# In-degrees from a stationary tile of ones, and keys of a fourth weight tile between the last transposes

## The chip, the cores and the metric

The kernel runs on one core of a Trainium2 chip. The metric is the device time of one execution in microseconds; the time before is the median of three runs. A separate execution was profiled, and every row quoted below is from it. Engines are called as the profile calls them: PE is TensorE's matmul, PEld its weight load, DVE is VectorE, ACT is ScalarE, POOL is GpSimd, SP is SyncE, whose queue issues most transfers.

## The reference

One layer of a graph network: 625 nodes of 1024 features in float32, and 20000 edges sorted by their destination. The layer's input is normalised, then two branches are added to it (a two-layer GraphSAGE and a linear attention), then a mixture of experts. What the change touches is the normalisation, the keys of the attention and the in-degrees:

```python
xn = _layernorm(x, axis=-1)
# graph branch
deg = segment_sum(ones, edge_dst, N)
deg_inv = 1.0 / maximum(deg, 1.0)
h = relu(sage(xn, src, dst, deg_inv, W_self0, W_neigh0, b0))
out = sage(h, src, dst, deg_inv, W_self1, W_neigh1, b1)
# sage: h @ W_self + (segment_sum(h[src], dst) * deg_inv[:, None]) @ W_neigh + b
# attention branch, 16 heads of 64
k = softmax(xn @ Wk over the nodes); q = softmax(xn @ Wq over a head) / 8
context = k^T v per head; attn = q context; attn @ Wo + bo
```

## The kernel before

**Numbers.** TensorE works in a float32 form of reduced precision, so each operand is split into a high and a low part (`split`: ScalarE casts the high part, VectorE subtracts it to get the low one), and each product is three products: high by high, high by low, low by high. Weights stream in tiles of 128x1024 (`Stream.next`, three raw and three split buffers); a load is issued as soon as a raw buffer has been split.

**Start.** The 625 nodes are five token tiles, four of 128 and one of 113 rows. For each, `first_stats` (VectorE) takes mean and variance, `first_scale` (VectorE, with a square root on ScalarE) turns them into scale and bias, `first_norm` normalises on VectorE or ScalarE, and `first_turn` transposes the tile on TensorE in two groups of four blocks (into `pst`) and splits it into `xnh` and `xnl`, with the features on partitions. The order of all these is written out by hand and kept on each engine (`keep`). While the last three token tiles are being prepared, TensorE multiplies the first three weight tiles of the keys with the first two token tiles: `keys_steps`, a step being half of a weight tile's features over some columns, 12 products. Here these are 256 columns (two token tiles); the remaining 370 columns of these three weight tiles follow behind the transposes.

**Keys and counting.** The steps go on through the eight tiles of Wk and the eight of W_self0 (columns 384 and 242 from the fourth tile on), each key tile being exponentiated (`keys_exp`) and transposed back (`keys_back`). `kbuf` is a ring of three key tiles. Between the steps VectorE builds one-hot rows of the edges (`one_hots`), of which TensorE makes the matrix of edge counts between source and destination (`count_group`, `pa`), with five source tiles packed into one number. `unpack` takes it apart into `ath`: source nodes on partitions, destinations along the row.

**In-degrees.** After the first half of the queries, `queries_step` runs between the quarters of the second half: it transposes the finished `q` of the first half, then in the first quarter calls `degrees` and in the second `look`. `degrees` multiplies each block of `ath` (as the stationary operand) with two columns of ones (`two`), so that the degrees of a destination tile stand on partitions; 25 products. `inverse_degrees` takes the reciprocal of the 128x5 result with one correction step (`recip`). `look` sums the degrees over everything and takes a maximum, and leaves in `rare` whether the packed counting may have overflowed; if so a slow path recounts, and all engines read `rare` before the attention's output. During the second half of the values, `inverse` spreads the inverse degrees over a row on all partitions (`dinv`) with five transposes and two copies on ScalarE. `dinv` scales the first layer's sums, `degs[:, 2]` the second layer's.

**Order.** PSUM has eight banks, handed out in turn under one tag; the queries' and the values' halves each hold five of them (`accs`). The scheduler orders each engine's instructions by priority except where they are kept; each engine runs its own in order.

Of the kernel before, what the change touches and what calls it, by code (L numbers as in the profile page):

```python
# [73 lines left out]
def gps_layer(ctx: ExitStack, tc: tile.TileContext, x, src, dst,  # L74
# [20 lines left out]
    def bank(name="ps"):  # L95
        return psum.tile([128, 512], F32, name=name, tag="ps")
# [5 lines left out]
    class Stream:  # L102
# [24 lines left out]
                self.raw[self.loaded] = r  # L127
                self.loaded += 1

        def next(self, eng=None, **order):  # L130
            if self.ready:
                return self.ready.pop(0)
            i = self.used
            self.used += 1
            self.load(max(i + self.ahead, i + 1))
            ap = self.todo[i]
            r = self.raw.pop(i)
            if self.pair is not None:
# [186 lines left out]
    def first_scale(a, b):  # L325
        inv_std(lnv[:T, a:b, 1], *(lnt[:T, i, a:b] for i in range(3)), order=keep)
        keep(nc.vector.scalar_tensor_tensor(lnt[:T, 1, a:b], lnv[:T, a:b, 0], -1.0, lnt[:T, 0, a:b],
                                            op0=ALU.mult, op1=ALU.mult))
# [26 lines left out]
        nc.tensor.transpose(psf[:, :EP], edges[:, 1, 0:1].to_broadcast([EP, 128]), ident[:EP, :EP])  # L355
        keep(nc.scalar.copy(first_dst, psf[:, :EP].rearrange("p (g j) -> p g j", g=NG)[:, :, 0]))

    shared = big.tile([128, 8 * NP], F32, name="shared", tag="big")
    kbuf = shared[:, 5 * NP:].rearrange("p (i s) -> p i s", s=NP)


    ksum = const.tile([128, KT], F32, name="ksum")
# [1 line left out]
    kscr = const.tile([128, KT], F32, name="kscr")  # L364

    def keys_back(o):
        ke = kbuf[:, o % 3, :N]
        for t0, n in ((0, NT - 1), (NT - 1, 1)):
            ps = bank("pskt").rearrange("p (a b) -> p a b", b=128)
            p = rows(t0)  # L370
            for t in range(n):
                nc.tensor.transpose(ps[p, t, :], ke[:, cols(t0 + t)], ident)
            nc.scalar.copy(knat[p, t0:t0 + n, o * 128:(o + 1) * 128], ps[p, :n, :])

    def keys_exp(o):
        ke = kbuf[:, o % 3, :N]
# [6 lines left out]

    def keys_step(s):
        o, i, h = s // 4, s // 2 % 2, s % 2
        if s < 12:
            o, i = s // 2 % 3, s // 6
        if (o, i, h) == (1, 1, 0):
            wks[3] = st.next()
        if i == 0 and h == 0 and 2 < o < 2 * KT - 1:  # L390
            wks[o + 1] = st.next()
        if h == 0:
            kps[0] = bank("psk")
        wh, wl = wks[o]
        c0, n = ((0, 2 * T), (2 * T, NP - 2 * T))[i] if o < 3 else SPARTS[i]
        c, ps = slice(c0, c0 + n), kps[0]
        for kt in range(4 * h, 4 * h + 4):
            nc.tensor.matmul(ps[:, :n], wh[:, kt, :], xnh[:, kt, c], start=kt == 0, stop=False)  # L398
            nc.tensor.matmul(ps[:, :n], wh[:, kt, :], xnl[:, kt, c], start=False, stop=False)  # L399
            nc.tensor.matmul(ps[:, :n], wl[:, kt, :], xnh[:, kt, c], start=False, stop=kt == KT - 1)  # L400
        if h == 1:
            n = min(n, N - c0)
            if o < KT:
                nc.scalar.copy(kbuf[:, o % 3, c0:c0 + n], ps[:, :n])
# [6 lines left out]
    def keys_steps(n):  # L411
        for _ in range(n):
            k = ks[0]
            ks[0] += 1
            if 8 <= k < 4 * KT + 8 and k % 4 == 0:
                keys_exp((k - 8) // 4)
            if 12 <= k < 4 * KT + 12 and k % 4 == 0:
                keys_back((k - 12) // 4)
            if k < 8 * KT:
                keys_step(k)  # L420

    def keys_weights(o):
        wks[o] = st.next(order=keep)


    with tc.high_priority():
        first_stats(0)
        first_stats(1)
        first_scale(0, 2)
        first_norm(0, nc.vector)  # L430
        keys_weights(0)
        first_norm(1, nc.scalar)
        first_turn(0)
        first_turn(1)
        first_stats(2)
        keys_weights(1)
        keep(nc.scalar.copy(edges, ei))
        keys_weights(2)
        keys_steps(2)
        turn_edges()  # L440
        keys_steps(2)
        first_stats(3)
        first_scale(2, 4)
        first_norm(2, nc.scalar)
        first_norm(3, nc.vector)
        keys_steps(2)
        first_stats(4)
        first_scale(4, 5)
        first_turn(2)
        first_norm(4, nc.scalar)  # L450
        first_turn(3)
        last = first_turn(4)


# [60 lines left out]
    knat = slot_n("knat")  # L515
    hself = slot_t("hself", F32)

    placed = 0
# [30 lines left out]
    def inverse_degrees():  # L549
        nc.vector.tensor_scalar(degs[:T, 1, :], degs[:T, 0, :], 1.0, None, op0=ALU.max)  # L550
        recip(degs[:T, 2, :], degs[:T, 1, :], degs[:T, 3, :])

    def degrees():
        ps = bank("psdg")
        for t in range(NT):
            for s in range(NT):
                nc.tensor.matmul(ps[rows(t), 2 * t:2 * t + 2], ath[rows(s), s, cols(t)], two[rows(s)],
                                 start=s == 0, stop=s == NT - 1)
        for a, b in ((0, NT - 1), (NT - 1, NT)):
            nc.vector.tensor_copy(degs[rows(a), 0, a:b],  # L560
                                  ps[rows(a), 2 * a:2 * b].rearrange("p (t k) -> p t k", k=2)[:, :, 0])
        inverse_degrees()

    rare = const.tile([1, 1], I32, name="rare")

    def look():


        nc.vector.reduce_sum(degs[:T, 4, 0:1], degs[:T, 0, :], axis=AX.X)
        ps = bank("psdm").rearrange("p (a b) -> p a b", b=128)  # L570
        for k in range(2):
            nc.tensor.transpose(ps[:1, k, :T], degs[:T, 4, k:k + 1], ident[:T, :T])
        few = const.tile([1, 2], F32, name="few")
        nc.vector.reduce_sum(few[:, 0:1], ps[:1, 0, :T], axis=AX.X)
        nc.vector.reduce_max(few[:, 1:2], ps[:1, 1, :T], axis=AX.X)
        nc.vector.tensor_scalar(few[:, 0:1], few[:, 0:1], float(E), None, op0=ALU.is_lt)
        nc.vector.scalar_tensor_tensor(rare, few[:, 1:2], 16.0, few[:, 0:1], op0=ALU.is_ge, op1=ALU.add)

    ard = dram.tile([NT * WIN, NP], F32, name="ard")
    atd = dram.tile([N, NP], F32R, name="atd")  # L580
# [1 line left out]
    def recount():  # L582
# [34 lines left out]
        for t in range(NT):  # L617
            pt = bank("psdt")
            for s in range(NT):
                al = tmp.tile([128, T], F32R, name="al", tag="tmp")  # L620
                nc.gpsimd.dma_start(al[rows(s), rows(t)], atd[cols(s), cols(t)])
                nc.tensor.matmul(pt[rows(t), :2], ath[rows(s), s, cols(t)], two[rows(s)], start=s == 0, stop=False)
                nc.tensor.matmul(pt[rows(t), :2], al[rows(s), rows(t)], two[rows(s)], start=False, stop=s == NT - 1)
            nc.vector.tensor_copy(degs[rows(t), 0, t:t + 1], pt[rows(t), 0:1])
        inverse_degrees()

# [76 lines left out]
    mid_ctx = ExitStack()  # L703
    midp = mid_ctx.enter_context(tc.tile_pool(name="midp", bufs=1))
    dinv = midp.tile([128, NP], F32, name="dinv")
# [618 lines left out]
```

## Time and profile before

| | |
|---|---|
| median of 3 runs | 1019.87 us (1019.27 to 1020.14) |
| profiled execution, whole | 1021.48 us |
| profiled execution, span from the first to the last instruction | 1019.5 us |
| mean granted TensorE clock | 0.998 |
| `degrees` on TensorE | 179.89 to 182.62 us |
| `look` on TensorE (two transposes) | 192.04 to 192.18 us |
| `inverse` on TensorE | 256.17 and 263.43 us |

A row of the timeline gives start and duration in us, engine, line, operation, the names written and read, the shapes, and in brackets the idle time before it and what ended that. Durations of a product include its tail, which lies beside the next one; the pace of products is read from the distance of their starts.

### The profile page before, as it was taken

The numbers are of one execution on the slowest core, as the hardware profiler recorded it, in microseconds if no ns is written. First come the engines' busy times: TensorE is split into PE (matmuls) and PEld (weight loads), VectorE is DVE, ScalarE is ACT, GpSimd is POOL, SyncE is SP. The second block draws the span as 40 slices with busy tenths as digits, with TensorE's granted clock in tenths as the row PEclk, the third lists the DMA queues.
The fourth block names the chain that finished last, engine by engine and source line by source line (L and its number), as shares of the span: only waits on it lengthen the run. The fifth ranks groups of instructions, "written<-read, shape, count | busy, mean of one in ns | idle before, by whom it ended". The sixth has DMA issues, their size and how long they took to land. (4 is left out here: it accounts for less than half of the span.)

```text
span 1019.5 us, 14780 instructions
## 1 busy us (share of the span) xinstructions
PE 999.7 (98%) x5557; PEld 862.4 (85%) x5557; DVE 595.5 (58%) x1207; ACT 394.7 (39%) x579; POOL 150.5 (15%) x206
## 2 busy tenths in 40 slices
PE   9999999999999999999999999999999989999998
PEld 6899998888888888888878999997978777887786
DVE  7999735462532335432337364458676788887681
ACT  4443232232311123122116242345646576766610
POOL 1000011110145100200001004103030043210130
PEclk9999999999999999999999999999999999999999
DMA  7122227574225421322220128476877798887961
GB/s 231 42 84 63 84 83 247 189 254 140 95 83 183 133 78 48 122 83 82 79 68 2 55 72 285 123 202 201 271 241 224 262 311 276 293 286 257 332 247 51
DMA packets 111464, 164.68 MB, mean 162 GB/s; under 512 B 5931, under 2 KB 63443, under 8 KB 111382
## 3 DMA queue, kind: packets, MB, share of 16 engines
q1 hardware_dynamic: 97734, 118.38, 36.9%
q0 software_dynamic: 13456, 45.08, 13.4%
q8 instruction: 47, 0.77, 0.3%
q14 instruction: 35, 0.29, 0.1%
q10 hardware_dynamic: 192, 0.16, 0.0%
HBM read 133.19 MB, written 30.42 MB: 160 GB/s over the span
## 5 line engine op out<-in xcount | busy, mean ns | idle before, releaser
L99 DVE TENSOR_TENSOR wlo<-wraw,whi 128x1024 fp32r<-128x1024 f32 x149 | 187.8, 1261 | 265.4 <-ACT whi L99 261.2
L99 ACT CAST whi<-wraw 128x1024 fp32r<-128x1024 f32 x149 | 156.6, 1051 | 286.1 <-PE psg L210 66.2
L1162 PE MATMUL pse<-xs,whi 128*128 128x448 f32 (+1 forms) x384 | 108.9, 357 | 0.0
L99 DVE TENSOR_TENSOR wlo<-wmore,whi 128x1024 fp32r<-128x1024 f32 x67 | 86.9, 1296 | 28.6 <-ACT whi L99 27.3
L1158 PE MATMUL pse<-xs,wlo 128*128 128x224 f32 (+1 forms) x384 | 89.6, 254 | 0.0
L99 ACT CAST whi<-wmore 128x1024 fp32r<-128x1024 f32 x67 | 70.4, 1051 | 48.4 <-PE psz L210 18.5
L398 PE MATMUL psk<-xnh,whi 128*128 128x384 f32 (+3 forms) x256 | 79.1, 313 | 0.4 <-ACT xnh L99 0.3
L399 PE MATMUL psk<-xnl,whi 128*128 128x384 f32 (+3 forms) x256 | 77.8, 307 | 0.8 <-DVE xnl L99 0.8
L400 PE MATMUL psk<-xnh,wlo 128*128 128x384 f32 (+3 forms) x256 | 77.7, 306 | 0.0
L1214 PE MATMUL psy<-wlo,he 128*128 128x512 f32 (+1 forms) x176 | 70.0, 398 | 3.3 <-DVE wlo L99 2.9
L1158 PEld LDWEIGHTS pse<-xs,wlo 128*128 128x128 f32 x384 | 72.0, 190 | 1.0
L1162 PEld LDWEIGHTS pse<-xs,whi 128*128 128x128 f32 x384 | 69.0, 189 | 2.4
L1213 PE MATMUL psy<-whi,he 128*128 128x512 f32 (+1 forms) x176 | 69.5, 395 | 0.0
L1215 PE MATMUL psy<-whi,he 128*128 128x512 f32 (+1 forms) x176 | 69.1, 392 | 0.0
L99 POOL TENSOR_TENSOR xs<-raw,xs 128x512 fp32r<-128x512 f32 (+2 forms) x24 | 35.5, 1501 | 118.9 <-ACT xs L99 98.6
L399 PEld LDWEIGHTS psk<-xnl,whi 128*128 128x128 f32 x256 | 48.5, 190 | 1.3 <-DVE xnl L99 1.3
L478 DVE TENSOR_SCALAR hot<-iota,srow,unit 125x128 f16<-125x128 f16 x160 | 49.4, 311 | 0.0
L398 PEld LDWEIGHTS psk<-xnh,whi 128*128 128x128 f32 x256 | 48.4, 190 | 0.9 <-ACT xnh L99 0.9
L400 PEld LDWEIGHTS psk<-xnh,wlo 128*128 128x128 f32 x256 | 48.4, 189 | 0.0
L1214 PEld LDWEIGHTS psy<-wlo,he 128*128 128x128 f32 (+1 forms) x176 | 31.8, 180 | 14.8 <-DVE wlo L99 6.6
L477 DVE TENSOR_SCALAR hot<-iota,edt 125x128 f16<-125x128 f16 x160 | 39.6, 251 | 4.1 <-PE pa L495 3.8
L1213 PEld LDWEIGHTS psy<-whi,he 128*128 128x128 f32 (+1 forms) x176 | 31.9, 181 | 10.1
(347 smaller groups left out, 2328.3 us busy)
## 6 DMA issues: line engine op xcount, KB each, us to landing
wraw<-in_L_ffn_w_dram SPq DMA_DIRECT2D x65, 512.0 KB, 5.0
wmore<-in_L_ffn_w_dram SPq DMA_DIRECT2D x63, 512.0 KB, 5.3
xsd<-zt POOLq DMA_DIRECT2D x9, 1024.0 KB
wraw<-in_L_gnn_W_self_dram SPq DMA_DIRECT2D x16, 512.0 KB, 3.8
wraw<-in_L_gnn_W_neigh_dram SPq DMA_DIRECT2D x16, 512.0 KB, 3.7
wraw<-_ffn_shared_gate_up_dram SPq DMA_DIRECT2D x16, 512.0 KB, 3.8
wraw<-in_L_mix_Wk_dram SPq DMA_DIRECT2D x8, 512.0 KB, 7.0
wraw<-in_L_mix_Wq_dram SPq DMA_DIRECT2D x8, 512.0 KB, 3.6
```

The source lines that it names most:

```text
L99: return (order(nc.scalar.copy(hi, srcap)), order((eng or nc.vector).tensor_sub(lo, srcap, hi.bitcast(F32))))
L398: nc.tensor.matmul(ps[:, :n], wh[:, kt, :], xnh[:, kt, c], start=kt == 0, stop=False)
L399: nc.tensor.matmul(ps[:, :n], wh[:, kt, :], xnl[:, kt, c], start=False, stop=False)
L400: nc.tensor.matmul(ps[:, :n], wl[:, kt, :], xnh[:, kt, c], start=False, stop=kt == KT - 1)
L477: nc.vector.tensor_scalar(h[:ET, :WIN], iota[:ET, :WIN], edst[e], None, op0=ALU.is_equal)
L478: return nc.vector.tensor_scalar(h[:ET, WIN:], iota[:ET, :WIN], srow[e], unit[e].bitcast(F32), op0=ALU.is_equal, op1=ALU.mult)
L1158: nc.tensor.matmul(ps[a][:, :n], wl[:, k, c], xs[:, kt, 0, :], start=False, stop=False)
L1162: nc.tensor.matmul(ps[a][:, :2 * n], wh[:, k, c], xs[:, kt], start=kt == 0, stop=kt == KT - 1)
L1213: nc.tensor.matmul(acc, h(kt, 0), wh[:, k, :], start=kt == 0, stop=False)
L1214: nc.tensor.matmul(acc, h(kt, 0), wl[:, k, :], start=False, stop=False)
L1215: nc.tensor.matmul(acc, h(kt, 1), wh[:, k, :], start=False, stop=kt == KT - 1)
```

## The change

Two things are changed. The in-degrees are made with a stationary tile of ones and `ath` as the moving operand, so that each sum comes out on all 128 partitions at once, along the row; the reciprocal is taken there, 128x314 and 128x312, and is `dinv` directly. `degrees` moves from the first to the third quarter of the queries' second half; `look` moves to the end of the values' first half, and now also turns `dinv` back into a column for `degs[:, 2]`. `inverse` is left for the slow path only.

At the start, a fourth weight tile of the keys is split early, into a buffer of its own (`fourth`), and its 256 early columns are multiplied in two steps between the transposes of the last three token tiles. `kbuf` becomes a ring of four in a buffer of its own, `keys_exp` and `keys_back` come two steps later, and the normalisation of the fifth token tile is placed ahead of the third one's transposes. The slot `knat` is taken earlier, and the one-hot rows begin with eight groups of four and not six.

```diff
-        def next(self, eng=None, **order):
+        def next(self, eng=None, into=None, **order):
...
-            if self.pair is not None:
+            if into is not None:
+                hi, lo = into
+            elif self.pair is not None:
...
-    shared = big.tile([128, 8 * NP], F32, name="shared", tag="big")
-    kbuf = shared[:, 5 * NP:].rearrange("p (i s) -> p i s", s=NP)
+    kbuf = big.tile([128, 4, NP], F32, name="kbuf", tag="big")
+
+    fourth = big.tile([128, 2, D], F32R, name="fourth", tag="big")
...
     def keys_step(s):
         o, i, h = s // 4, s // 2 % 2, s % 2
-        if s < 12:
-            o, i = s // 2 % 3, s // 6
+        if s < 16:
+            o, i = s // 2 % 4, s // 8
         if (o, i, h) == (1, 1, 0):
-            wks[3] = st.next()
-        if i == 0 and h == 0 and 2 < o < 2 * KT - 1:
+            wks[4] = st.next()
+        if i == 0 and h == 0 and 3 < o < 2 * KT - 1:
             wks[o + 1] = st.next()
...
-        c0, n = ((0, 2 * T), (2 * T, NP - 2 * T))[i] if o < 3 else SPARTS[i]
+        c0, n = ((0, 2 * T), (2 * T, NP - 2 * T))[i] if o < 4 else SPARTS[i]
...
-            if 8 <= k < 4 * KT + 8 and k % 4 == 0:
-                keys_exp((k - 8) // 4)
-            if 12 <= k < 4 * KT + 12 and k % 4 == 0:
-                keys_back((k - 12) // 4)
+            if 10 <= k < 4 * KT + 10 and k % 4 == 2:
+                keys_exp((k - 10) // 4)
+            if 14 <= k < 4 * KT + 14 and k % 4 == 2:
+                keys_back((k - 14) // 4)
...
     def keys_weights(o):
-        wks[o] = st.next(order=keep)
+        wks[o] = st.next(into=(fourth[:, 0, :], fourth[:, 1, :]) if o == 3 else None, order=keep)
...
         keys_steps(2)
         turn_edges()
-        keys_steps(2)
         first_stats(3)
         first_scale(2, 4)
         first_norm(2, nc.scalar)
         first_norm(3, nc.vector)
-        keys_steps(2)
+        keys_weights(3)
+        keys_steps(4)
         first_stats(4)
         first_scale(4, 5)
+        first_norm(4, nc.scalar)
         first_turn(2)
-        first_norm(4, nc.scalar)
+        keys_steps(1)
         first_turn(3)
+        keys_steps(1)
         last = first_turn(4)
...
+    knat = slot_n("knat")
     with tc.high_priority():
-        for _ in range(6):
+        for _ in range(8):
             keys_steps(1)
...
-    two = const.tile([128, 2], F32R, name="two")
-    nc.vector.memset(two.bitcast(F32), 1.0)
+    ones = const.tile([128, 128], F32R, name="ones")
+    nc.vector.memset(ones.bitcast(F32), 1.0)
+    dinv = const.tile([128, NP], F32, name="dinv")
...
     def degrees():
-        ps = bank("psdg")
-        for t in range(NT):
-            for s in range(NT):
-                nc.tensor.matmul(ps[rows(t), 2 * t:2 * t + 2], ath[rows(s), s, cols(t)], two[rows(s)],
-                                 start=s == 0, stop=s == NT - 1)
-        for a, b in ((0, NT - 1), (NT - 1, NT)):
-            nc.vector.tensor_copy(degs[rows(a), 0, a:b],
-                                  ps[rows(a), 2 * a:2 * b].rearrange("p (t k) -> p t k", k=2)[:, :, 0])
-        inverse_degrees()
+        for i, (c0, n) in enumerate(PARTS):
+            ps = bank("psdg")
+            for s in range(NT):
+                nc.tensor.matmul(ps[:, :n], ones[rows(s), :], ath[rows(s), s, c0:c0 + n], start=s == 0, stop=s == NT - 1)
+            nc.vector.reduce_sum(few[:, i:i + 1], ps[:1, :n], axis=AX.X)
+            deg = tmp.tile([128, 2, PARTS[0][1]], F32, name="deg", tag="tmp")
+            nc.vector.tensor_scalar(deg[:, 0, :n], ps[:, :n], 1.0, None, op0=ALU.max)
+            recip(dinv[:, c0:c0 + n], deg[:, 0, :n], deg[:, 1, :n])
...
     def look():
-        nc.vector.reduce_sum(degs[:T, 4, 0:1], degs[:T, 0, :], axis=AX.X)
-        ps = bank("psdm").rearrange("p (a b) -> p a b", b=128)
-        for k in range(2):
-            nc.tensor.transpose(ps[:1, k, :T], degs[:T, 4, k:k + 1], ident[:T, :T])
...
+        ps = bank("psdm")
+        for t in range(NT):
+            nc.tensor.transpose(ps[rows(t), t:t + 1], dinv[:1, cols(t)], ident[:1, :1])
+        for a, b in ((0, NT - 1), (NT - 1, NT)):
+            nc.vector.tensor_copy(degs[rows(a), 2, a:b], ps[rows(a), a:b])
+        nc.tensor.transpose(ps[:1, 128:128 + T], degs[:T, 4, 1:2], ident[:T, :T])
+        nc.vector.reduce_max(few[:, 2:3], ps[:1, 128:128 + T], axis=AX.X)
+        nc.vector.tensor_add(few[:, 0:1], few[:, 0:1], few[:, 1:2])
...
     def queries_step(u):
...
-        if u == 0:
+        if u == 2:
             degrees()
-        elif u == 1:
-            look()
...
     def values_step(half, u):
         if half == 0:
...
-        elif u > 1:
-            inverse(*((0, NT - 1), (NT - 1, 1))[u - 2])
+            if u == 3:
+                look()
```

More of the change, by code (lines that the diff above doesn't have):

```diff
@@ L366, in keys_back @@
     def keys_back(o):
-        ke = kbuf[:, o % 3, :N]
+        ke = kbuf[:, o % 4, :N]
         for t0, n in ((0, NT - 1), (NT - 1, 1)):
@@ L375, in keys_exp @@
     def keys_exp(o):
-        ke = kbuf[:, o % 3, :N]
+        ke = kbuf[:, o % 4, :N]
         mx = small.tile([128, 2], F32, name="mx")
@@ L403, in keys_step @@
             if o < KT:
-                nc.scalar.copy(kbuf[:, o % 3, c0:c0 + n], ps[:, :n])
+                nc.scalar.copy(kbuf[:, o % 4, c0:c0 + n], ps[:, :n])
             else:
@@ L514, in gps_layer @@
                 one_hots(4)
-    knat = slot_n("knat")
     hself = slot_t("hself", F32)
@@ L551, in inverse_degrees @@
         recip(degs[:T, 2, :], degs[:T, 1, :], degs[:T, 3, :])
+    few = const.tile([1, 4], F32, name="few")
     def degrees():
-        ps = bank("psdg")
-        for t in range(NT):
+        for i, (c0, n) in enumerate(PARTS):
+            ps = bank("psdg")
             for s in range(NT):
-                nc.tensor.matmul(ps[rows(t), 2 * t:2 * t + 2], ath[rows(s), s, cols(t)], two[rows(s)],
-                                 start=s == 0, stop=s == NT - 1)
-        for a, b in ((0, NT - 1), (NT - 1, NT)):
-            nc.vector.tensor_copy(degs[rows(a), 0, a:b],
-                                  ps[rows(a), 2 * a:2 * b].rearrange("p (t k) -> p t k", k=2)[:, :, 0])
@@ L566, in look @@
     def look():
-        nc.vector.reduce_sum(degs[:T, 4, 0:1], degs[:T, 0, :], axis=AX.X)
-        ps = bank("psdm").rearrange("p (a b) -> p a b", b=128)
-        for k in range(2):
-            nc.tensor.transpose(ps[:1, k, :T], degs[:T, 4, k:k + 1], ident[:T, :T])
-        few = const.tile([1, 2], F32, name="few")
-        nc.vector.reduce_sum(few[:, 0:1], ps[:1, 0, :T], axis=AX.X)
-        nc.vector.reduce_max(few[:, 1:2], ps[:1, 1, :T], axis=AX.X)
+        ps = bank("psdm")
+        for t in range(NT):
+            nc.tensor.transpose(ps[rows(t), t:t + 1], dinv[:1, cols(t)], ident[:1, :1])
@@ L576, in look @@
+        for a, b in ((0, NT - 1), (NT - 1, NT)):
[3 more added lines that the diff above has]
+        nc.vector.tensor_add(few[:, 0:1], few[:, 0:1], few[:, 1:2])
         nc.vector.tensor_scalar(few[:, 0:1], few[:, 0:1], float(E), None, op0=ALU.is_lt)
-        nc.vector.scalar_tensor_tensor(rare, few[:, 1:2], 16.0, few[:, 0:1], op0=ALU.is_ge, op1=ALU.add)
+        nc.vector.scalar_tensor_tensor(rare, few[:, 2:3], 16.0, few[:, 0:1], op0=ALU.is_ge, op1=ALU.add)
@@ L621, in recount @@
                 nc.gpsimd.dma_start(al[rows(s), rows(t)], atd[cols(s), cols(t)])
-                nc.tensor.matmul(pt[rows(t), :2], ath[rows(s), s, cols(t)], two[rows(s)], start=s == 0, stop=False)
-                nc.tensor.matmul(pt[rows(t), :2], al[rows(s), rows(t)], two[rows(s)], start=False, stop=s == NT - 1)
+                nc.tensor.matmul(pt[rows(t), :2], ath[rows(s), s, cols(t)], ones[rows(s), :2], start=s == 0, stop=False)
+                nc.tensor.matmul(pt[rows(t), :2], al[rows(s), rows(t)], ones[rows(s), :2], start=False, stop=s == NT - 1)
             nc.vector.tensor_copy(degs[rows(t), 0, t:t + 1], pt[rows(t), 0:1])
@@ L704, in gps_layer @@
     midp = mid_ctx.enter_context(tc.tile_pool(name="midp", bufs=1))
-    dinv = midp.tile([128, NP], F32, name="dinv")
     def values_step(half, u):
```

## The prediction

> **What bounds the kernel now.** I read the page's busy shares first: TensorE is busy for nearly the whole span, so only what shortens TensorE's own queue, or fills a hole in it, moves the end.
>
> ```profile
> span 1019.5 us, 14780 instructions
> PE 999.7 (98%) x5557; PEld 862.4 (85%) x5557; DVE 595.5 (58%) x1207; ACT 394.7 (39%) x579; POOL 150.5 (15%) x206
> ```
>
> So I went to the two places that the change touches. The first is the start, in TensorE's timeline (start, duration, line, idle time before it) and then ScalarE's:
>
> ```profile
> 23.21 0.28 PE L400 MATMUL psk<-xnh,wlo 128*128 128x256 f32 x1
> 23.54 1.97 PE L282 MATMUL pst<-ident,xts 128*128 128x128 f32 x16
> 27.12 0.70 PE L282 MATMUL pst<-ident,xts 113*128 113x113 f32 x5 [1.62 <-ACT xts L336]
> ...
> 27.91 0.51 PE L282 MATMUL pst<-ident,xts 113*128 113x113 f32 x3
> 28.52 0.77 PE L398 MATMUL psk<-xnh,whi 128*128 128x370 f32 x3
> 29.53 0.44 PE L399 MATMUL psk<-xnl,whi 128*128 128x370 f32 x1 [0.23 <-DVE xnl L99]
> ```
>
> ```profile
> 25.83 1.24 ACT L336 ACTIVATE xts<-xts,lnt 113x1024 f32<-113x1024 f32 x1
> 26.98 2.02 ACT L99 CAST xnh<-pst 128x512 fp32r<-128x512 f32 x4
> ```
>
> The early keys run out at 23.33. Until the keys of the other columns run steadily, about 29.0 (29.53 less three products of 0.17 started early), only 24 transposes of 0.11 and a small one run: 2.75 of 5.7 us. Some 2.9 us are lost, mostly to the fifth tile's normalisation on ScalarE.
>
> The second place is the in-degrees: TensorE's timeline, then the same stretch by windows (per window: busy time of PE, PEld, DVE, ACT, POOL, then the granted clock and DMA).
>
> ```profile
> 179.10 1.03 PE L669 MATMUL psqt<-ident,q 128*128 128x128 f32 x8
> 179.89 2.87 PE L557 MATMUL psdg<-two,ath 128*128 128x2 f32 x25
> 182.62 0.47 PE L208 MATMUL psq<-whi,xnh 128*128 128x512 f32 x1
> ...
> 185.90 0.63 PE L208 MATMUL psq<-whi,xnh 128*128 128x512 f32 x1
> ```
>
> ```profile
> 180.00:182.00 2.00, 2.00 (x21) 2.00 (x20) 1.62 (x4) 1.88 (x4) 0.30 (x1) 1.00 0.56 197
> 182.00:184.00 2.00, 2.00 (x13) 1.78 (x13) 1.20 (x5) 0.00 (x0) 0.00 (x0) 0.86 1.03 276
> 184.00:186.00 2.00, 2.00 (x6) 1.52 (x6) 2.00 (x10) 0.00 (x0) 0.00 (x0) 0.50 0.93 301
> 186.00:188.00 2.00, 2.00 (x9) 1.59 (x8) 0.29 (x3) 0.00 (x0) 0.47 (x2) 0.78 0.78 256
> ```
>
> 25 products with two moving columns hold TensorE from 179.89 to 182.62, 2.73 us or 0.109 each. Right behind them the granted clock is halved. From 183.40 to 187.04 nine products of 512 columns take 3.64 us, where 0.227 each (187.04 to 187.27, and so on) would make 2.04: 1.60 us lost. It is the one clear dip of the clock in the trace.
>
> **The change, part by part.**
>
> *In-degrees.* Removed from TensorE: the 25 narrow products, 2.73; the two transposes of `look`, 0.14; and in `inverse` four transposes that push the next product from 256.17 to 256.52, 0.35, and one of 0.10. Added: ten products with 314 or 312 moving columns. The products of 256 columns start 0.120 apart (14.80 to 14.92), those of 370 0.170 apart (29.97 to 30.14); a line between gives 0.145, so 1.45 us. `look` now has six tiny transposes: by the narrow products 0.109 each, by the old ones 0.07; I take 0.65 us. Together -3.42 + 2.10 = -1.32 us. The dense products also leave nothing that looks like the stretch before the dip: -1.60 us.
>
> *What hides the added VectorE work.* VectorE gets, in a row, two sums, two maxima from PSUM, two reciprocals, and a correction of three instructions for each. Rows near: 128x314 from PSUM takes 0.48 (L824), scalar-tensor on 625 columns 0.81 and so some 0.45 for 314, tensor-scalar 0.49 for 626 and so 0.3. A reciprocal that wide is not in the trace:
>
> ```profile
> L294 DVE RECIPROCAL qm<-qm 128x8 f32<-128x8 f32 x8 | 1.5, 196 | 0.0
> L261 DVE RECIPROCAL lnt<-lnt 128x1 f32<-128x1 f32 x5 | 0.8, 162 | 1.2 <-ACT lnt L259 1.2
> L824 DVE TENSOR_TENSOR hr<-psag,dinv 128x314 f32<-128x314 f32 x8 | 3.9, 482 | 2.2 <-PE psag L811 2.2
> ```
>
> From below it costs what a plain pass costs, 0.48; from above, if all 0.196 us were per element, 7.7 us. The slope between the two reciprocal rows, 34 ns over 7 elements, gives 0.16 + 313 x 0.0049 = 1.7 us; I take that, as both rows are the same operation. The chain is then some 6.5 us and starts behind a weight split. Counted from the start of the half's last quarter, VectorE is free for the query softmax at 7.1 us; in the old trace it began at 2.0 (201.59 against 199.6). Behind it wait the softmax, so the PSUM banks of `accs`, so the values' products, then the transposes of `q` and the splits of Wv. With passes of 0.6 us I get the second bank back at 11.2, where TensorE asks for it at 12.3 (one quarter of 6.85 and four groups of 1.37); the first transposed `q` at 14.1 against 15.5, as the schedule puts it eight products into the next quarter; the third weight split at 20.2 against 22. So it is hidden, with 1.1 us to spare, and each microsecond beyond reaches the end. If the reciprocals cost as little as a plain pass, the spare is 3.5 us and the time the same. I charge 0. [...]
>
> `look` is now later, at the end of the values' first half. The read of `rare` moves on the load queue from behind the fourth load of Wv to behind the second of Wo. The first loads of Wo were issued from 231.13 on, one per 6.9 us; the look's result is due about 238, so nothing waits. Two copies of `dinv` leave ScalarE, which had idle time there.
>
> *Fourth key tile.* Two early steps are added, 24 products of 256 columns at 0.120, 2.88 us. The same products leave the later stage, whose shape changes from 384 and 242 columns to 256 and 370, the same 626 in sum: worth under 0.1. The weights' load is issued at the same place in the load queue, and all transfers of that time had landed by 23.6. What moves is the tile's cast and split: the cast now stands on ScalarE behind the third tile's normalisation, the split on VectorE before the fifth tile's statistics; and the fifth tile's normalisation now stands on ScalarE ahead of all the `xnh` casts. I walk the new order with the old durations. The root of tiles 2 and 3 no longer stands behind a PSUM copy: statistics done 19.87, scale 21.24 (22.24 before), third tile normalised 22.4, cast of the fourth weights 22.4 to 23.44, its split 23.5 to 24.6, statistics of tile 4 24.6 to 26.15 (started 22.97 before), its scale by 27.45, its normalisation 27.5 to 28.7. Only then come four casts of 0.5, a PSUM copy of 0.35 and two casts: 32.0, against 29.0 (26.98 + 2.02). So the later keys start 2.9 us later, minus the 2.88 already done, with the VectorE halves in step behind them: I take -0.1 us. From below, the extra keys could fill the whole hole: -2.8. From above, the new hole (29.65 to 31.55 by this walk, with 0.5 before its transposes) could cost a clock dip: +1.6. The value is near the middle because each row in the walk is a measured one.
>
> [...]
>
> After the start VectorE lags its keys by 1.6 us more (start 2.75 later, one split of 1.15 already done). Old slack covers it: one-hot rows finished some 7 us before the first count at 47.48.
>
> **Sum.** -1.32 - 1.60 - 0.1 = -3.0 us. Against the profiled execution, span 1019.5 of 1021.48 us, that makes a span of 1016.5. The timed runs have a median of 1019.87, 1.6 below the profiled execution, for which I have two readings: the profiler's own cost, or a dip that timed runs miss. By the first, 1019.87 - 3.0 = 1016.9.
>
> **Rivals.**
>
> A, the dip is not in the timed runs: the trace shows one dip in one execution. For it: the 1.6 us just named equals the dip's price. Against it: three runs within 0.9 us show no two levels. Time: 1016.9 + 1.6 = 1018.5.
>
> B, the early keys fill the hole: the walk is pessimistic and the casts run ahead of the fifth tile. For it: ScalarE is idle for some 3 us there by the walk. Against it: the written order keeps them behind. Time 1016.9 - 2.7 = 1014.2.
>
> C, slower: the wide reciprocals become the bound. Place: between in-degrees and query softmax on VectorE. They use up the 1.1 us and then push the values' products; from 3.75 us each (4.1 us more than I took) the kernel is slower than before. For it: nothing so wide is measured; against it: the small rows' slope. At 7.7 each: 12.0 - 1.1 = 10.9 us of stall, 1027.8.
>
> D, the clock dips in the new hole: 1018.5 as well.
>
> **Numbers.** Forecast 0.52, A 0.20, B 0.09, C 0.14, D 0.05. A difference under 0.2% (2.0 us) can't be told from no change here: faster means below 1017.83. The forecast spreads by some 0.9 us, so most of it, all of B and a little of A are faster: 0.57. A, D and the forecast's upper end: 0.30. C, nearly all: 0.13. The range reaches from a partly filled hole, 1015.0, past A and D to 1019.9, where a stall of 1.4 us on A would lie.
>
> **What would show it.** In-degrees right: ten products starting 0.145 apart, a clock of 1.00 behind them. Reciprocals: their row at 128x314, near 1.7 us; and no idle time of TensorE in the values' first quarters. Start right: the fifth tile's normalisation near 27.5, keys of 370 columns steady from near 32. It is wrong if the dip returns elsewhere, if TensorE waits on `q` or a bank, or if the hole at the start is under 1 us or over 4.

## The result and the profile after

The changed kernel takes 1022.72 us (median of 19 runs, 1020.5 to 1023.95) where the kernel before takes 1020.52 us (median of 19, 1019.27 to 1021.63): a ratio of 1.0023, interval 1.0017 to 1.003. It is slower by some 2 us; forecast were 3 us less.

The head of the changed kernel's page has 32 TensorE instructions fewer (16 products and their 16 weight loads), all from the in-degrees:

```profile
span 1020.2 us, 14750 instructions
PE 998.6 (98%) x5541; PEld 860.8 (84%) x5541; DVE 604.4 (59%) x1213; ACT 395.3 (39%) x577; POOL 149.7 (15%) x206
```

The in-degrees in the timeline of TensorE and VectorE (start, duration, engine, line, operation, names, shapes):

```profile
195.48 1.70 PE L566 MATMUL psdg<-ath,ones 128*128 128x314 f32 x10
...
198.81 2.09 DVE L296 RECIPROCAL dinv<-deg 128x314 f32<-128x314 f32 x1
...
201.55 2.08 DVE L296 RECIPROCAL dinv<-deg 128x312 f32<-128x312 f32 x1
...
203.83 0.39 PE L210 MATMUL psv<-whi,xnh 128*128 128x512 f32 x1
```

The next product behind the ten starts at 197.02, so they hold TensorE for 1.54 us. The values' first product starts at 203.83 with no wait; before it was 206.3. The windows of that stretch (busy time of PE, PEld, DVE, ACT, POOL, then clock, DMA share, GB/s) have no dip of the clock left:

```profile
180.00:186.00 6.00, 6.00 (x32) 5.08 (x30) 5.33 (x13) 2.54 (x4) 1.16 (x2) 1.00 0.61 212
186.00:192.00 6.00, 6.00 (x33) 4.96 (x32) 1.22 (x1) 2.02 (x3) 1.16 (x2) 1.00 0.63 189
192.00:198.00 6.00, 6.00 (x34) 5.16 (x33) 1.51 (x2) 1.49 (x2) 0.45 (x2) 1.00 0.63 248
```

The start, again from the timeline: the fifth tile's normalisation, the six casts behind it (the PSUM copy lies between), and the first keys of 370 columns.

```profile
28.06 1.25 ACT L338 ACTIVATE xts<-xts,lnt 113x1024 f32<-113x1024 f32 x1 [1.01 <-DVE lnt L329]
...
29.21 2.02 ACT L99 CAST xnh<-pst 128x512 fp32r<-128x512 f32 x4
...
31.37 1.02 ACT L99 CAST xnh<-pst 128x452 fp32r<-128x452 f32 x2
...
32.01 0.77 PE L401 MATMUL psk<-xnh,whi 128*128 128x370 f32 x3 [1.35 <-ACT xnh L99]
32.96 0.44 PE L402 MATMUL psk<-xnl,whi 128*128 128x370 f32 x1 [0.18 <-DVE xnl L99]
```

So far everything is near the forecast. At the experts' last product (psy) the changed kernel is still ahead, by 4.1 us (954.47 against 958.59). Then it loses this lead in one place, ahead of the shared expert's second product (psz). Its timeline there, and that of the kernel before:

```profile
954.47 0.39 PE L1222 MATMUL psy<-whi,he 128*128 128x512 f32 x1
959.86 0.58 PE L210 MATMUL psz<-whi,sth 128*128 128x512 f32 x1 [5.01 <-issue]
960.24 0.63 PE L211 MATMUL psz<-wlo,sth 128*128 128x512 f32 x1
960.67 0.63 PE L212 MATMUL psz<-whi,stl 128*128 128x512 f32 x1
```

```profile
958.59 0.39 PE L1215 MATMUL psy<-whi,he 128*128 128x512 f32 x1
960.43 0.47 PE L208 MATMUL psz<-whi,sth 128*128 128x512 f32 x1 [1.45 <-DVEq L1262]
960.74 0.40 PE L209 MATMUL psz<-wlo,sth 128*128 128x512 f32 x1
960.97 0.40 PE L210 MATMUL psz<-whi,stl 128*128 128x512 f32 x1
```

Between these two products stands the branch over the overflow loop, `if n_over > 0` (L1262 before, L1269 after), which isn't entered here. Before, TensorE's sequencer waits 1.45 us there for the other engines. After, it waits 5.01 us "for issue", that is, for nothing that the profile names, be it a product, a transfer or a semaphore. Behind it the products start 0.43 us apart instead of 0.23 (960.24 to 960.67, before 960.74 to 960.97), so the clock there is about halved. The windows of both, the changed kernel's first:

```profile
954.00:960.00 6.00, 0.99 (x5) 0.70 (x4) 3.33 (x3) 2.19 (x3) 0.54 (x1) 0.96 0.78 244
960.00:966.00 6.00, 6.00 (x21) 4.77 (x21) 0.00 (x0) 0.00 (x0) 3.76 (x4) 0.76 0.97 338
```

```profile
954.00:960.00 6.00, 4.98 (x22) 3.75 (x20) 5.08 (x5) 5.12 (x7) 0.56 (x1) 1.00 0.97 335
960.00:966.00 6.00, 5.57 (x25) 4.61 (x26) 1.46 (x2) 0.55 (x1) 1.44 (x2) 1.00 0.77 252
```

The cost is 5.01 - 1.45 = 3.6 us of halt, and 6 x (0.04 + 0.24) = 1.7 us of clock.

In the view of the DMA queues (packets, MB, share) two queues are named "instruction" in the changed kernel:

```profile
q8 instruction: 46, 0.75, 0.3%
q14 instruction: 35, 0.29, 0.1%
```

The first fits TensorE: its 46 packets of 0.016 MB stand beside 5541 products and 5541 weight loads, some 240 instructions for a packet (an estimate from these counts). No view names the engine. The packet of this queue that comes nearest ahead of psz, in the half microsecond from 957.5, lies behind the last product:

```profile
q8 instruction: 1, 0.02, 12.6%
```

In the kernel before, the packet lies at 955.5, some 3 us ahead of its last product:

```profile
q8 instruction: 1, 0.02, 12.2%
```

So the reading to test: the next packet of TensorE's code had already begun when TensorE reached the branch in the one kernel (955.5 against 958.59), and not in the other (957.5 against 954.47).

A second difference helped the changed kernel. Before, TensorE also halts for issue in the shared expert's first product (psup), 1.85 us in all, and after it doesn't. The kernel before:

```profile
625.54 0.34 PE L222 MATMUL psup<-xfh,wlo 128*128 128x384 f32 x1 [0.56 <-issue]
...
626.28 0.27 PE L222 MATMUL psup<-xfh,wlo 128*128 128x242 f32 x1 [0.17 <-issue]
627.67 0.44 PE L220 MATMUL psup<-xfh,whi 128*128 128x384 f32 x1 [1.12 <-issue]
```

### The profile page after: what moved, and what is told of

Its sections match the earlier page's. It is cut to its first block, busy times and chain, and to the rows that moved or that the text cites. A ratio compares the mean times of both kernels' runs of the same rounds, so it can differ in the third digit from the quotient of the medians.

```text
span 1020.2 us, 14750 instructions
## 1 busy us (share of the span) xinstructions
PE 998.6 (98%) x5541; PEld 860.8 (84%) x5541; DVE 604.4 (59%) x1213; ACT 395.3 (39%) x577; POOL 149.7 (15%) x206
## 5 line engine op out<-in xcount | busy, mean ns | idle before, releaser
L401 PE MATMUL psk<-xnh,whi 128*128 128x384 f32 (+3 forms) x240 | 74.6, 312 | 1.7 <-ACT xnh L99 1.7
L402 PE MATMUL psk<-xnl,whi 128*128 128x384 f32 (+3 forms) x240 | 73.6, 307 | 0.7 <-DVE xnl L99 0.7
L403 PE MATMUL psk<-xnh,wlo 128*128 128x384 f32 (+3 forms) x240 | 73.5, 306 | 0.0
L401 PEld LDWEIGHTS psk<-xnh,whi 128*128 128x128 f32 x240 | 45.4, 190 | 2.2 <-ACT xnh L99 2.2
L402 PEld LDWEIGHTS psk<-xnl,whi 128*128 128x128 f32 x240 | 45.5, 190 | 1.2 <-DVE xnl L99 1.2
L403 PEld LDWEIGHTS psk<-xnh,wlo 128*128 128x128 f32 x240 | 45.4, 189 | 0.0
```

## The experiments

Three theories were set against each other. Theory 1: the halt ahead of psz comes from where the branch falls in the packets of TensorE's program. Theory 2: it comes from what the earlier arrival meets there, wherever the code stands. Theory 3: the loss is a clock dip in the hole at the start. The expectations of e1 to e4 were written before theory 2 was stated, and call the dip at the start theory 2; from e5 on the numbers are as here. The runs were made in four groups, on three chips, with 5 to 12 executions each; each ratio is against runs of the kernel before on the same chip, whose medians were 1021.55 (e1 to e4), 1022.88 (e5 to e8), 1018.98 (e9 to e12) and 1021.99 (e13, e14). So only ratios are compared across groups.

### e1 to e4: the two kernels again, and the two parts alone

e1 is the kernel before, e4 the changed kernel. e2 has the hunks of `degrees`, `look`, `ones` and `dinv` alone, e3 the others alone.

> The kernel before, unchanged, for its spread of times and of mean granted clocks over many executions. Theory 1 (the changed kernel loses in front of the last stage: TensorE there waits 5.0 us for nothing that the profile shows, against about 1.5 us before, and a halved clock follows): ratio 1.00, mean clocks near 0.998 in nearly all executions, and a gap in front of the products of psz of about 1.5 us. Theory 2 (the clock dips at the start, in the new hole at 29 to 33 us): also 1.00 and clocks near 0.998. Theory 3 (chance: the halt is not tied to the code): the gap in front of psz varies from execution to execution, clocks vary as much as in the changed kernel.

> Only the in-degrees from a stationary tile of ones, with the start as before. Theory 1, if the halt is tied to how many instructions TensorE has passed (32 fewer, all from this part): the halt in front of psz of about 5 us and mean clocks of 0.994 to 0.996 are here, ratio 1.002. Theory 2: no halt, clocks 0.998 or more, ratio about 0.997, some 3 us faster. Theory 3: anything between, with executions of both kinds.

> Only the keys of the fourth tile between the transposes, with the in-degrees as before. Theory 1: the same number of TensorE instructions as before, so no longer halt in front of psz; ratio 1.000 within 0.001, clocks as before. Theory 2: the dip at the start is here, clocks 0.994 to 0.996, 2 to 4 us slower. Theory 3: as in the kernel before.

> The changed kernel again, for a second profile. Theory 1: again a halt of TensorE of 4 to 6 us in front of psz with a halved clock behind it; ratio 1.002. Theory 2: a halved clock between 29 and 40 us in this profile, if its mean clock is 0.994 to 0.996. Theory 3: the halt is gone or elsewhere.

Measured: e1 1022.39 us (ratio 1.001, 1.0 to 1.0021), e2 1022.8 (1.0007, 0.9997 to 1.0016), e3 1021.58 (1.0003, 0.9994 to 1.0012), e4 1022.8 (1.0004, 0.9995 to 1.0013). The medians alone decide little: the ratio of 1.002 expected of e2 and e4 did not come, and on this chip the changed kernel can't be told from the kernel before. The low clocks expected (0.994 to 0.996) came in 6 of 11 runs of e2 and in 9 of 11 of e4. What the halt costs is therefore read from e5 and e6, not from here. The waits do decide: TensorE waits ahead of psz 1.5 us for a queue in e1 and 1.4 in e3, as before, and 4.5 us for issue in e2 and 4.1 in e4, as after. So the halt came with the in-degrees part, which is the part that removes 32 instructions. The halt at psup (1.9 us) is in e1 and e3 and in neither of the others.

### e5: the changed kernel with 32 instructions more at its beginning

```
-WARM = 34
+WARM = 50
...
-        nc.tensor.matmul(psw, cold[:, :128], cold, ...)
+        nc.tensor.matmul(psw[:, :348], cold[:, :128], cold[:, :348], ...)
```

> The changed kernel with 50 warm-up products of 348 columns in place of 34 of 512: the same columns (17400 for 17408), but 32 more TensorE instructions (16 products, 16 weight loads), so that everything behind stands at the same place of TensorE's program as in the kernel before. Theory 1 (the halt in front of psz comes from where the branch falls in the fetched blocks of TensorE's program): psz waits 1.4 to 1.5 us for DVEq as before instead of 4 to 5 us for issue, no halved clock at 960 to 966, and the halt of about 2 us at psup comes back. Sum from the changed kernel's 1022.7: -3.5 (5.0 to 1.5) -1.4 (six us at 0.76) +2.0 = about 1019.8. Theory 2 (the halt comes from what the earlier arrival meets there, the weights in flight, wherever the code stands): the halt stays at 4 to 5 us, 1022.7. Theory 3 (the loss is a clock dip in the hole at the start): 1022.7, with a clock under 0.9 at 24 to 36 us.

1017.32 us, ratio 0.995 (0.9936 to 0.9965). TensorE's waits in e5 (total, times, longest) and the timeline at the branch:

```profile
PE psk L401 <- ACT xnh L99: 1.7, 2, 1.3
...
PE psz L210 <- DVEq L1269: 1.5, 1, 1.5
```

```profile
954.90 0.39 PE L1222 MATMUL psy<-whi,he 128*128 128x512 f32 x1
956.74 0.47 PE L210 MATMUL psz<-whi,sth 128*128 128x512 f32 x1 [1.45 <-DVEq L1269]
```

The arrival is as early as in the changed kernel, yet the halt is gone and the clock from 960 to 966 is 1.00: theory 2 falls. The one miss: the halt at psup did not come back. Theory 3 has its sign in this trace, though. A dip of the clock that the changed kernel's profile lacks now stands behind the hole at the start:

```profile
24.00:30.00 6.00, 5.17 (x40) 4.48 (x39) 3.84 (x14) 3.35 (x7) 0.00 (x0) 1.00 0.32 89
30.00:36.00 6.00, 4.93 (x18) 4.64 (x19) 5.86 (x23) 1.27 (x4) 0.00 (x0) 0.72 0.01 3
```

### e6: the same shift, but only behind the experts

```
+    tiny = const.tile([128, 128], BF16, name="tiny")
+    nc.vector.memset(tiny, 0.0)
...
             if i == 0:
                 turn(1)
+            if i == 4 and last:
+                psn = bank("psnone")
+                for _ in range(16):
+                    nc.tensor.matmul(psn[:, :16], tiny, tiny[:, :16], start=True, stop=True)
```

> The changed kernel with 16 tiny bf16 products (16 columns, into a bank that nobody reads) between the weight tiles of the last expert's second product, so that only the branch and the last stage stand 32 TensorE instructions later; psup stands where it does in the changed kernel. Theory 1: the fetch of the block that holds the branch's target starts before the branch is reached; psz waits about 1.5 us, no halt at psup either, and the tiny products cost 0 to 1.6 us (16 of at most 0.1 us, partly inside the waits of psy for wlo, 3.1 us in all). Sum: 1022.7 -3.5 -1.4 +0.5 = about 1018.3. Theory 2: the halt stays at 4 to 5 us, 1022.7 to 1024.

1017.89 us, ratio 0.9954 (0.9939 to 0.9968); psz waits 1.7 us for a queue, none for issue:

```profile
PE psz L210 <- ACTq L1275: 1.7, 1, 1.7
```

The 16 tiny products start within 0.4 us. So it isn't the longer or other warm-up that helped in e5.

### e7, e8 and e11: the hole at the start

```
...
         keys_steps(4)
+        low = []
+        for g in range(2):
+            ps = bank("pst").rearrange("p (a b) -> p a b", b=128)
+            ...
+            keep(nc.scalar.copy(h, ps))
+            low.append((xnl[:, 4 * g:4 * g + 4, cols(2)], ps, h.bitcast(F32)))
         first_stats(4)
         first_scale(4, 5)
         first_norm(4, nc.scalar)
-        first_turn(2)
+        for lo in low:
+            keep(nc.vector.tensor_sub(*lo))
```

e7 has this alone, e8 with e6's tiny products, e11 with e5's warm-up.

> The changed kernel with the third token tile's two casts emitted ahead of the fifth tile's statistics and normalisation (its subtractions behind them on VectorE), so that ScalarE casts in the idle time before 28 us. The later keys' first product waits 1.35 and 0.18 us in the changed kernel; with the casts of 1.0 us out of the way it starts about 1.1 to 1.3 us earlier. Theory 1 alone: the halt in front of psz stays 4 to 5 us, and the time is 1.2 us less, about 1021.5. Theory 3 (part of the loss in the timed runs is a clock dip behind the hole at the start): more than that, 2 to 3 us less.

> Both: the 16 tiny products in the last expert and the third tile's casts ahead of the normalisation. Theory 1: the two gains add, about 1017.1; psz waits about 1.5 us and no TensorE wait is named issue. Theory 2: 1021.5, the halt stays.

> The 50 short warm-up products and the third tile's casts ahead of the normalisation, without tiny products. Theory 1: as e8 (1016.0) without what the tiny products cost (0 to 0.6 us), about 1015.5; psz waits 1.5 us, no TensorE wait is named issue, no dip at 30 to 36 us.

e7 takes 1021.2 us (0.9984, 0.9974 to 0.9995): psz still waits 4.2 us for issue, and the keys' wait for the casts falls from 1.7 to 0.7 us, as both expected. By the ratios it is 2.0 us under e4 (1.0004), nearer to the 2 to 3 of theory 3 than to the 1.2 of theory 1 alone. e8 takes 1015.98 (0.9934, 0.9919 to 0.9948), e11 1015.15 (0.9962, 0.9949 to 0.9975), e8 under e6 by 1.9 us on one chip. Part of that is a clock dip: e6's trace has one at the start (0.76 from 30 to 36 us). Neither trace of e8 or e11 has a window of 6 us with a clock under 0.98 from 12 us until TensorE's last products. These two are faster than both kernels.

### e9 and e10: the in-degrees alone, both kernels moved

Both have e5's warm-up; e9 on the in-degrees part alone, e10 on the kernel before.

> The in-degrees part alone (as in e2), with 50 warm-up products of 348 columns. Theory 1: the halt of 4.5 us in front of psz becomes 1.5 us and the halved clock behind it goes: the in-degrees part then shows what it is worth, 3 to 5 us under the kernel before, about 1017 to 1018. Set beside e5_pad_early (1017.3), which has the start part as well, it prices the start part: 0 by the walk of the start (2.83 us later, 2.88 done early), plus 1.3 to 1.6 on the other side if the hole in front of the later keys has a clock dip behind it. Theory 2: halt as in e2, no gain.

> The kernel before with 50 warm-up products of 348 columns: everything behind stands 32 TensorE instructions later. A control for e5: the shorter products themselves do nothing, and the branch's block was fetched in time already (its packet came 3.1 us ahead of the last product; now about 6.5 us). Theory 1: no change, psz waits 1.4 to 1.5 us, ratio 0.999 to 1.001, or 2 us less if the halt at psup depends on its place in the program. Rival (the gain of e5 is from the warm-up, not from the place of the branch): 4 to 5 us less, ratio 0.995.

e9 takes 1017.41 us (0.9988, 0.9979 to 0.9996), e10 1020.62 (1.0011, 1.0002 to 1.002). So the pad gains nothing for the kernel before, whose psz waits 1.6 us and whose halt at psup is gone, though the 2 us that this was to bring did not come. With both moved the medians differ by 3.2 us. Of these, 1.4 us are there at the values' first product (204.7 against 206.1 us), and 1.7 at the end of psup (670.4 against 672.1); the rest comes in the experts, where e10 takes 1.4 us longer from the first to the last product of psy (265.9 against 264.5 us). Why is open, but the profile of the kernel before has 264.3 us there, so these 1.4 us belong rather to e10 than to the in-degrees. Against the kernel before itself e9 gains 1.2 us by its ratio, less than the 3 to 5 expected. The comparison of e9 with e5 that was to price the start part decides nothing: their times are equal (1017.41 and 1017.32 us), their ratios are not (0.9988 and 0.995), as the kernel before differs by 3.9 us between the two chips.

e10's windows show where its clock dipped:

```profile
24.00:30.00 6.00, 4.05 (x27) 3.14 (x26) 5.04 (x16) 4.42 (x8) 0.00 (x0) 0.96 0.00 0
30.00:36.00 6.00, 6.00 (x29) 6.00 (x29) 4.54 (x22) 1.00 (x2) 0.00 (x0) 0.76 0.00 0
180.00:186.00 6.00, 6.00 (x45) 5.46 (x44) 4.82 (x13) 2.54 (x4) 1.16 (x2) 1.00 0.83 263
186.00:192.00 6.00, 6.00 (x34) 4.96 (x32) 1.70 (x11) 0.80 (x1) 0.82 (x2) 1.00 0.85 264
```

The old 25 narrow products are in it, and no dip behind them; the dip stands at the old start instead.

### e12 and e14: how far the code must be moved

e12 has 38 warm-up products of 458 columns (8 instructions more than the changed kernel), e14 has 42 of 414 (16 more).

> The changed kernel with 38 warm-up products of 458 columns: only 8 TensorE instructions more, a quarter of e5's step. In e5 the code packet came 3.4 us ahead of the last product before the branch; 32 instructions are 16 products of 0.217 us, 3.5 us, so without a step it would be due 0.1 us behind it, which is where the changed kernel halts. Theory 1, with a threshold at the branch: 8 instructions bring it 0.9 us, to some 0.8 us ahead of the last product, so it is asked for in time: the halt goes or is under 2.5 us, 1017.5 to 1019.5. If the block must be there several us earlier: halt 4 us, 1022.

> The changed kernel with 42 warm-up products of 414 columns: 16 TensorE instructions more, between e12 (8: halt 4.4 us) and e5 (32: none). The code packet of e5 came 3.4 us ahead of the last product, that of e6 and e8 2.5 us; 16 instructions fewer than e5's are 8 products of 0.217 us, 1.7 us: about 1.7 us ahead. Theory 1 with a threshold under 1.7 us: no halt, as e5, 4 to 5 us under e12. Theory 1 with a threshold of 1.7 to 2.5 us: halt 4 us, as e12.

e12 takes 1023.44 us (1.005, 1.0037 to 1.0063), e14 1017.91 (0.9961, 0.9949 to 0.9973). The waits at the branch, e12 and then e14:

```profile
PE psz L210 <- PEq L1269: 4.4, 1, 4.4
```

```profile
PE psz L210 <- ACTq L1269: 1.7, 1, 1.7
```

8 instructions leave the halt, 16 remove it. The packet comes 0.3 to 0.8 us ahead of the last product in e14, not 1.7 as I had worked out, and that is enough. So the halt of e12 can't be put down to a packet that must be there several us earlier, as its second expectation had it; the first, which placed the packet 0.8 us ahead, had the time of the packet wrong. In these points it is a switch and not a slope: with the packet 0.3 to 0.8 us ahead of the last product the wait is 1.72 us (e14), with it 1.4 to 1.9 us behind, 4.43 us (e12). What sets the time at which a packet begins is in no view.

### e13: the converse, the kernel before made to halt

```
-WARM = 34
+WARM = 27
...
         nc.tensor.matmul(psw, cold[:, :128], cold, ...)
+        if 4 < i < 22:
+            for _ in range(7):
+                nc.tensor.matmul(psw[:, :16], cold[:, :128], cold[:, :16], start=False, stop=False)
```

> The converse of e5. The kernel before with 27 warm-up products of 512 columns and 119 of 16 columns among them (each 0.03 us, as 16 such took 0.4 us in e6), in place of 34: 224 TensorE instructions more. [...] Theory 1: the kernel before, in-degrees by narrow products and old start, halts 4 to 5 us for issue in front of psz, with a halved clock behind it, and its code packet comes 2 to 3 us behind the last product ahead of the branch: 3.0 + 1.7 us more than before, ratio 1.004 to 1.005. Rival (the halt comes with the earlier arrival or with the new in-degrees, and the place only helps): psz waits 1.5 us, ratio 1.000.

1028.25 us, ratio 1.0063 (1.005 to 1.0077). The timeline of e13 at the branch:

```profile
959.37 0.39 PE L1218 MATMUL psy<-whi,he 128*128 128x512 f32 x1
963.30 0.47 PE L208 MATMUL psz<-whi,sth 128*128 128x512 f32 x1 [3.54 <-PEq L1265]
```

With the old in-degrees and the old start, the kernel before halts for 3.54 us, a little less than the 4 to 5 expected, and its clock is 0.89 and 0.82 from 960 to 972. Its first key starts 1.0 us late, since the warm-up is longer (14.3 against 13.3); that is in the ratio too, which is above the 1.004 to 1.005 expected. The packet comes about 1 us behind the last product, not 2 to 3. So the place decides, and not the new code. That 224 more stands for 30 to 35 fewer is an estimate from the traces: from the packet at 40.2 us to the ninth behind it, at 212.3, the kernel before has 2289 TensorE instructions, and the changed one 2331 from 36.6 to 213.8, so some 254 and 259 for a packet. The 240 of the whole program is less, as it holds gaps such as the two from 263.0 to 286.8 us before (169 and 107).

All traces in one table. "Place" is the number of TensorE instructions ahead of the branch, against the kernel before; e13's 224 is 30 to 35 fewer if counted from the next packet on, by the estimate above. The packet is given by the half microsecond in which it begins.

| kernel | place | packet | last product | psz waits |
|---|---|---|---|---|
| before | 0 | 955.5 | 958.6 | 1.45 |
| e1 | 0 | 956.5 | 959.0 | 1.52 |
| e3 | 0 | 957.5 | 960.8 | 1.45 |
| e5 | 0 | 951.5 | 954.9 | 1.45 |
| e9 | 0 | 951.5 | 955.0 | 1.45 |
| e11 | 0 | 949.5 | 952.5 | 1.45 |
| e6 | 0 | 952.5 | 955.1 | 1.67 |
| e8 | 0 | 951.5 | 954.0 | 1.67 |
| e10 | +32 | 951.0 | 958.1 | 1.59 |
| e14 | -16 | 954.5 | 955.3 | 1.72 |
| e12 | -24 | 957.0 | 955.6 | 4.43 |
| after | -32 | 957.5 | 954.5 | 5.01 |
| e4 | -32 | 959.0 | 957.0 | 4.07 |
| e2 | -32 | 957.0 | 954.8 | 4.51 |
| e7 | -32 | 955.0 | 952.9 | 4.17 |
| e13 | +224 | 960.0 | 959.4 | 3.54 |

In all ten with the short wait, the packet is ahead of the last product; in all six with the long one, it is behind, and psz starts 2.4 to 3.4 us after the time given for the packet. That the packet is the cause and not a companion of the halt is shown by no run; that the place makes the halt is what e5, e6, e12, e14 and e13 show.

## Why the prediction was wrong

**In-degrees on TensorE: right.** Ten products took 1.54 us where 1.45 stood. The five tiny transposes of `look` and the one behind them cost about 0.6 us, where 0.65 stood. At the values' first product the gain against the kernel before is 2.5 us, in an execution that was already 0.6 us late at its first key. Between e9 and e10, which both have no dip there, it is 1.4 us, where the products ahead of the values make 2.73 + 0.14 - 1.54 = 1.33. One sum in the prediction is off: the products removed add up to 3.32 us and not 3.42, so the term should have been -1.22 and the whole -2.9.

**Reciprocals: right in kind, mis-sized.** 2.09 and 2.08 us where 1.7 stood. The query softmax began 7.75 us after the start of the last quarter (204.77 less 197.02) where 7.1 stood, and the 1.1 us to spare covered it: psv starts without a wait. Rival C is out.

**Start: right.** Normalisation at 28.06 (27.5), keys at 32.01 (near 32). e3 alone gives a ratio of 1.0003, so the part is worth nothing that can be measured, as the -0.1 us said. Rival B is out for the order as written; the value of the hole is what e7, e8 and e11 took from it.

**The clock dip behind the narrow products: the wrong kind of term.** I took -1.60 us as bound to that place. In the traces a dip of this size, 1.7 us summed over its windows, moves about: behind the narrow products in the kernel before, e1 and e3; at the start in e10 and e13, which have the same narrow products and no dip behind them, and in e2, whose start is that of the kernel before. Three traces (e8, e11, e14) have none. As far as these traces go, removing one hole is worth a dip only if no other hole takes it. Rivals A and D each held a part of this, but neither as it is.

**The sum: the step that failed.** "that makes a span of 1016.5" carries -3.0 us unchanged to the end, with nothing charged for the stages behind the two places that the change was taken to touch. It does touch them: with 32 instructions fewer, every later one stands elsewhere in TensorE's program, and the packet of code that began 3 us ahead of the last product before the branch (955.5 against 958.59) began 3 us behind it (957.5 against 954.47). With that place came 3.6 us of halt at the branch and 1.7 us of clock behind it. No rival had this, and the range ended at 1019.9. With the place restored, e5 has a span of 1015.8 us, near the 1016.5 of the prediction, but in part by luck. Its dip isn't gone, it stands at the start (1.7 us worse than the sum), while the halt at psup is gone (1.85 us) and its first key starts 0.5 us earlier than before (12.79 against 13.28); the sum had neither.

**The timed runs against the profiled one.** The profile of the changed kernel has one dip and a mean clock of 0.998. Of its 19 runs, 11 had 0.994 and 4 had 0.996, which in the profiles of e12 and of e2 and e4 goes with three dips and two; these 15 took 1023.0 on average, the 4 others 1021.2. So the median is also longer by dips that this one profile doesn't show. The traces of e2 (24 to 36 us) and e12 (30 to 42 us, besides those at the branch) show that the start is one such place, and e4 has one at 834 to 840. Where they lay in the timed runs can't be seen.

## What to carry to other kernels

A changed number of instructions moves every later branch to another place in the program: 32 fewer made the wait at the branch 5.01 us here, where it was 1.45. If a branch lies on the bounding engine's path, look whether the packet of the instruction queue comes ahead of it (in these 16 traces the wait was 1.45 to 1.72 us with it ahead, 3.54 to 5.01 with it behind), and if not, try a few tiny instructions in front of it (16 products of 16 columns took 0.4 us here, and the wait fell from 5.0 to 1.7 us). Charge a clock dip to the execution and not to a hole: the dip of 1.7 us stood behind the in-degrees in the kernel before and at the start in e10, with the same code at both places, so removing the hole where one trace shows it need not pay. And a wait for "issue" that is new in a stage which the change doesn't touch is a reason to compare the places in the program before looking at data.

## What the runs showed of the hardware that was not expected

- The halt at the branch works as a switch: 3.5 to 5.0 us with the place at -24 or -32 (e13 counted so), 1.45 to 1.7 us from -16 to +32.
- TensorE also waited "for issue" without a branch: the 1.85 us at psup, in straight code, with a DMA share of 1.03 to 1.08 from 621 to 630 us (before, e1 and e13). That code was late there is not shown: in the kernel before, the queue of packets for TensorE has none that begins between 612 and 634 us. Such halts came in the kernel before, e1, e3 and e13, at two places of the program, and not in e5, which stands at the same place as before. So neither place nor load alone decides that one. ScalarE stood still as well: in these four traces its activation of the gate's sums (psga) starts 4.3 us behind the last product that writes them, in the twelve others 0.1 to 1.1 us. The cause stays open.
- Clock dips come in portions: summed over its windows, one is 1.7 us, or 0.0017 of the span (1.68 in the kernel before and e10, 1.74 in e1 and e9). The profiles have none (e8, mean clock 1.000; e11 and e14, 0.999), one (before, after, e10: 0.998), two (e2, e4: 0.996) or three (e12: 0.994).
- The start with its 24 transposes has a dip behind it in some executions and none in others. In the kernel before the clock was 1.00 from 23.4 to 30.2 us, with the transposes in it, and from 30 to 36 us; in e1 it was 1.00 as well. With the same order at the start, e9 and e10 have 0.75 and 0.76 from 30 to 36 us, and e2 has 0.87 and 0.85 from 24 to 36 us. So the one trace that I had did not show whether the place has a dip.
